# Second attention of a two-layer decoder: the product of probabilities and values issued half a step later, ahead of the next transposes

## The chip, the cores and the metric

The kernel runs on one core of one Trainium2 chip. The metric is the device time of one execution in microseconds (us). Everything is computed in 32-bit floating point. The engines are written as the profile names them: PE (TensorE, matmuls), PEld (its weight loads), DVE (VectorE), ACT (ScalarE), POOL (GpSimd) and SP (SyncE, which here issues all DMAs of the part that matters).

## What is computed

Four blocks follow each other, each with a residual and a layer norm: a first attention (low-rank, 32 heads), a gated feed-forward block, a second attention, and a linear layer with eight routed low-rank experts. The activations are 4 sequences of 256 rows, 512 wide. The change lies in the second attention:

```python
q = einsum('bsd,de->bse', x, wq).reshape(B, S, 32, 192)[..., :128]
kv = einsum('bsd,de->bse', x, wkv)            # keys and values, 32 heads of 128
scores = einsum('bqhd,bkhd->bhqk', q, k) * 192 ** -0.5
scores = where(causal, scores, -1e30)
probs = softmax(scores, axis=-1)
attn = einsum('bhqk,bkhd->bqhd', probs, v).reshape(B, S, 4096)
out = einsum('bse,ed->bsd', attn, wo)
```

## The kernel before

**Three kinds of work share the second attention.** (1) The projections to queries, keys and values and the output projection are done by a fast block scheme: seven products of blocks in place of eight, at two levels, so that each product is followed by additions. A *stage* is one group of seven products; `seven` (L787) turns it into seven *units*. A unit is a few matmuls (L874 for queries and keys, L969 for values, L1059 for the output projection) into one of three PSUM banks `ps_b`, and one eviction of that bank, on ACT (L800) or on DVE (L803; L1068 for the output projection). Later additions of whole blocks, which read the intermediate results kept in `x`, run on POOL (L895). The differences of weight blocks are made on POOL too (L136 to L139, and for the output projection L1034 to L1037). (2) The attention itself runs in 128 *steps*, one for each of 32 heads and 4 sequences. (3) DMAs, all issued in order by SP.

**A step of the attention** has five parts.

- `scores1` (L1093): two products of queries and keys into the bank `ps_s`. They are issued through the helper `mm`, so their line is L63. Then DVE adds the mask (L1100) and takes two maxima (L1104), and ACT takes two exponentials with their sums (L1108).
- `softmax1` (L1116): DVE takes the reciprocals of the sums (L1118), ACT scales the probabilities `pr` (L1120).
- `transposes1` (L1123): PE turns three 128x128 blocks of `pr` into the bank `ps_t` (L1126), and DVE copies them to `pT` (L1128).
- `output1` (L1131): PE multiplies the values `v` with `pT` into the bank `ps_o` (L1135 and L1136), ACT copies the result to `att` (L1138), and SP stores it to the DRAM buffer `attd` (L1139).
- Between these, the units that the step has been given. Heads are taken in 8 groups of 4, so a group has 16 steps. While group g is in its steps, the units of the projections of group g+1 are spread over 32 half steps (`todo`, L1221 to L1224). In the last group the units are the rest of the projections (L874), and then the first two rounds of the output projection (`so[0]` and `so[1]`, L1059).

In each step the loop (L1218 to L1244) issues: the scores of this step; the units of the first half; the transposes of the step before; the units of the second half; the product with the values of the step before; the scaling of this step's probabilities.

**The order on each engine.** The framework that builds the kernel puts the instructions of each engine into one fixed order ahead of time. It goes by the order of the code and by when it expects operands and buffers to be ready. So an instruction can stand somewhat earlier or later in an engine's queue than in the code. At run time every queue is worked off in that order.

**Buffers that matter.** `ps_s` and `ps_t` have two banks each, `ps_o` has one. `pT` has two buffers, `pr` and `att` have three. The values `v` have two buffers, so that `att0`, the buffer that later takes the attention output back for the output projection, takes the place of `v[6]`, the values of the last group but one (heads 24 to 27).

**The handover in the last group.** After the first step of the last group, the loop calls `o_load(0)` (2 MB from `attd` into `att0`, L1022), the weight loads of the first two rounds (L836 into `ws`, L839 into `w`), the weight differences of round 0 (`ahead`, L1034 to L1037 on POOL, and L1044 to L1047 for the other side, in round 0 on DVE, into `to`), `o_load(1)` (into `xo`), and `back(0)`, which reads `x` back from DRAM (L1179).

```python
            for i in range(GH * B):
                h, b = GH * g + i // B, i % B
                pr, sm = scores1(h, b)
                ...
                if pending:
                    output1(pending[0], pending[1], pT)
                pending = (h, b, softmax1(pr, sm))
                if last and i == 0:
                    o_load(0)
```

Of the kernel before, what the change touches and what calls it, by code (L numbers as in the profile page):

```python
# [38 lines left out]
def tile_decoder2(ctx: ExitStack, tc: tile.TileContext, a: dict, out: bass.AP):  # L39
# [13 lines left out]
    def bank(tag, shape=(P, 512)):  # L53
        return ps["pool"].tile(list(shape), F32, tag=tag, name=f"ps_{tag}", bufs=ps["bufs"][tag])
# [112 lines left out]
    with tc.tile_pool(name="l0", bufs=1) as l0, tc.tile_pool(name="l0b", bufs=2) as l0b:  # L167
# [280 lines left out]
        pending, flush = [], []  # L448
# [313 lines left out]
    with banks("ps1", b0=1, b1=1, b2=1, s=2, t=2, o=1), \  # L762
# [249 lines left out]
        def o_load(r):  # L1012

            if r == 0:
                ov[0] = l1.tile([P, GH, N], F32, tag="v", name="att0")
                xo = l1x.tile([P, 5 * GH, Q], F32, tag="x2o", name="xo")
                ov[1] = xo[:, :4 * GH].rearrange("p (h t) c -> p h (t c)", t=4)
                odd = [xo[:, 4 * GH:], *(wts.tile([P, 4, Q], F32, tag=f"x2{i}", name=f"xo{i}", bufs=1) for i in (2, 0))]
                ov["c"] = ([
                    l1x.tile([P, 2, HN], F32, tag=f"t{i}", name=f"to{i}") for i in (1, 3, 5)  # L1020
                ], [t.rearrange("p (h t) c -> p h (t c)", t=2) for t in odd])
            nc.sync.dma_start(out=ov[r % 2], in_=attd[r])  # L1022
# [70 lines left out]
        def scores1(h, b):  # L1093

            sc = bank("s", (P, 3, P))
            q0, q1 = bass.ts(2 * b, P), bass.ts(2 * b + 1, P)
            mm(sc[:, 0, :], [(qn[h][:, q0], kn[h][:, q0])])
            mm(sc[:, 1:3, :], [(qn[h][:, q1], kn[h][:, b * S:(b + 1) * S])])
            diag = sc[:, 0:3:2, :]
            nc.vector.tensor_tensor(diag, diag, mask, ALU.add)  # L1100
            nmx = small.tile([P, 2], F32, name="nmx")
            parts = (slice(0, 1), slice(1, 3))
            for qt, pt in enumerate(parts):
                nc.vector.tensor_reduce(nmx[:, qt:qt + 1], sc[:, pt, :], AX.XY, ALU.max, negate=True)  # L1104
            pr = l1.tile([P, 3, P], F32, tag="pr", name="pr", bufs=3)
            sm = small.tile([P, 2], F32, name="sm")
            for qt, pt in enumerate(parts):
                nc.scalar.activation(  # L1108
                    pr[:, pt, :], sc[:, pt, :], AF.Exp, bias=nmx[:, qt:qt + 1],
                    accum_out=sm[:, qt:qt + 1],  # L1110
                )
            if b == B - 1:
                free.extend((where[(True, h)], where[(False, h)]))
            return pr, sm

        def softmax1(pr, sm):  # L1116
            rc = small.tile([P, 2], F32, name="rc")
            nc.vector.reciprocal(rc, sm)  # L1118
            for qt, pt in enumerate((slice(0, 1), slice(1, 3))):
                nc.scalar.activation(pr[:, pt, :], pr[:, pt, :], AF.Copy, scale=rc[:, qt:qt + 1])  # L1120
            return pr

        def transposes1(pr):  # L1123
            tp = bank("t", (P, 3, P))
            for i in range(3):
                nc.tensor.transpose(tp[:, i, :], pr[:, i, :], ident)  # L1126
            pT = l1.tile([P, 3, P], F32, tag="pT", name="pT")
            nc.vector.tensor_copy(pT, tp)  # L1128
            return pT

        def output1(h, b, pT):  # L1131
            g, hh = divmod(h, GH)
            hv = slice(hh * DV, (hh + 1) * DV)
            po = bank("o", (P, S))
            nc.tensor.matmul(po, v[g][:, 2 * b, hv], pT[:, 0:2, :], start=True, stop=False)  # L1135
            nc.tensor.matmul(po[:, P:], v[g][:, 2 * b + 1, hv], pT[:, 2, :], start=False, stop=True)  # L1136
            att = l1.tile([P, S], F32, tag="att", name="att", bufs=3)
            nc.scalar.copy(att, po)  # L1138
            nc.sync.dma_start(out=attd[g][:, hh, b * S:(b + 1) * S], in_=att)  # L1139
# [36 lines left out]
        def back(t0):  # L1176

            for t in (t0, t0 + 2):
                nc.sync.dma_start(out=x[:, t:t + 2, :], in_=xd[:, t:t + 2, :])  # L1179
# [22 lines left out]
        def units_of(stages):  # L1202

            units = []
            for st in stages:
                def begin(st=st):
                    for key in ("load", "att", "next"):
                        if key in st:
                            st[key]()

                (u, w), rest = st["units"][0], st["units"][1:]
                units += [((lambda begin=begin, u=u: (begin(), u())), w), *rest]
            return units

        for u, _ in units_of(groups[0]):
            u()
        pending = None
        for g in range(NG):  # L1218
            last = g == NG - 1
            units = units_of(rest + so[0] + so[1]) if last else units_of(groups[g + 1])  # L1220
            total, at, todo = sum(w for _, w in units), 0, {}  # L1221
            for u, w in units:
                todo.setdefault((2 * at + w) * 4 * GH * B // (4 * total), []).append(u)
                at += w  # L1224
            for i in range(GH * B):
                h, b = GH * g + i // B, i % B
                pr, sm = scores1(h, b)
                for u in todo.get(2 * i, ()):
                    u()
                if pending:  # L1230
                    pT = transposes1(pending[2])
                for u in todo.get(2 * i + 1, ()):
                    u()
                if pending:
                    output1(pending[0], pending[1], pT)
                pending = (h, b, softmax1(pr, sm))
                if last and i == 0:
                    o_load(0)
                    even.extend((free.pop(0), free.pop(0)))
                    for r in range(2):  # L1240
                        so[r][0]["w"]()
                    so[0][0]["ahead"]()
                    o_load(1)
                    back(0)  # L1244
        output1(pending[0], pending[1], transposes1(pending[2]))


        iscale = 1.0 / math.sqrt(DK)
# [162 lines left out]
```

## Time and profile before

| what | value |
|---|---|
| time, median of 3 runs | 1682.19 us (1681.59 to 1682.57) |
| time of the profiled execution | 1681.63 us |
| its span, first to last instruction | 1679.6 us |
| mean granted clock of TensorE | 0.997 |
| steps of groups 0 to 6, up to the handover | about 880 to 1342 us of the span |
| handover in the last group | about 1342 to 1400 us |
| rest of the last group's steps | about 1400 to 1453 us |

The profile is one execution. Its page gives the busy time of each engine and the chain of work that ended last, which is followed back from the end. The trace behind it also gives, for any window, the instructions in order of time (the timeline), the chain of waits in order of time, the issues of DMAs with the time until they landed, and who waited for whom. Columns of the timeline are: start in us, duration in us, engine, line, operation, output and inputs, shape, count. A matmul in 32-bit numbers shows as two instructions, so "L1135 x2" is one product of the code. Ends of matmuls are modelled by the profiler, so starts are the safer reading.

### The profile page before, as it was taken

To read this page: it belongs to the slowest core of one execution; us is meant where nothing else is said; L and a number is where in the kernel's file an instruction comes from. 1 tells how busy PE (TensorE), PEld (TensorE's weight loads), DVE (VectorE), ACT (ScalarE), POOL (GpSimd) and SP (SyncE) were. 2 spreads that over 40 slices of the span, in tenths; PEclk is the share of its full clock that TensorE was granted. 3 is DMA by queue.
4 is the path that set the end of the run, shared out by engine and by line. 5 is a ranking of instruction groups with operands and counts; after the bars stand their busy time and mean duration, and the time that the engine had idled before them with its cause. 6 is when DMAs were issued, how large, how long until landed. Compare 5 with 4: busy or idle time off the path is not lost.

```text
span 1679.6 us, 24076 instructions
## 1 busy us (share of the span) xinstructions
PE 1644.5 (98%) x7954; PEld 1294.9 (77%) x7954; DVE 1064.9 (63%) x2345; ACT 700.8 (42%) x2070; POOL 1104.5 (66%) x1330
## 2 busy tenths in 40 slices
PE   8999999999999998999999999999999999999998
PEld 5566666666488887888878888888888878888854
DVE  3577777777745536677777666666666775433454
ACT  1566666667422202111125555555555553200043
POOL 1988888881437445786667767677676777689530
PEclk9999999999999999999999999999999999999999
DMA  9465555451312002687524334253342344443000
GB/s 345 152 211 215 217 199 205 175 194 50 108 43 77 13 26 73 200 262 248 187 76 128 115 98 144 71 178 118 95 140 73 122 176 161 155 151 125 26 18 33
DMA packets 96251, 226.88 MB, mean 135 GB/s; under 512 B 10272, under 2 KB 53792, under 8 KB 90112
## 3 DMA queue, kind: packets, MB, share of 16 engines
q1 hardware_dynamic: 94464, 224.54, 38.9%
q8 instruction: 63, 1.03, 0.3%
q10 hardware_dynamic: 1664, 0.81, 0.2%
q14 instruction: 60, 0.49, 0.1%
HBM read 140.38 MB, written 84.93 MB: 134 GB/s over the span
## 4 chain that ended last, share of the span: by engine, by line
PE 88%; DVE 7%; POOL 2%; DMA 1%; ACT 1%; issue 1%; DVEq 0%; SPq 0%; POOLq 0%; ACTq 0%
PE ps_b L874 19%; PE ps_s L63 13%; PE ps_b L1059 11%; PE ps_b L969 5%; PE ps_o L1135 4%; PE ps_o L396 3%; PE ps_s L612 3%; PE ps_t L379 3%; PE ps_p L294 3%; PE ps_t L1126 2%; PE ps_o L63 2%; PE ps_t L969 2%; PE ps_o L612 2%; PE ps_p L612 2%; PE ps_b L63 2%; PE ps_p L302 2%
## 5 line engine op out<-in xcount | busy, mean ns | idle before, releaser
L1108 ACT ACTIVATE pr<-ps_s,nmx 128x128 f32<-128x128 f32 (+1 forms) x256 | 105.0, 416 | 105.0 <-DVE nmx L1104 101.9
L355 ACT ACTIVATE pr<-ps_s,ebias 128x256 f32<-128x256 f32 x256 | 117.7, 472 | 48.5 <-DVE ebias L350 46.9
L1068 DVE TENSOR_TENSOR x<-ps_b,x 128x512 f32<-128x512 f32 x96 | 66.2, 690 | 105.0 <-PE ps_b L1059 97.5
L63 PE MATMUL ps_s<-kT,qh 128*128 128x256 f32 x512 | 129.1, 393 | 1.1 <-ACT pr L355 1.1
L1120 ACT ACTIVATE pr<-pr,rc 128x128 f32<-128x128 f32 (+1 forms) x256 | 103.8, 448 | 56.6 <-DVE rc L1118 55.0
L1100 DVE TENSOR_TENSOR ps_s<-ps_s,mask 128x256 f32<-128x256 f32 x128 | 55.2, 431 | 106.5 <-PE ps_s L63 106.5
L63 PEld LDWEIGHTS ps_s<-kT,qh 128*128 128x128 f32 x512 | 91.5, 189 | 37.6 <-issue 20.2
L803 DVE SCALAR_TENSOR_TENSOR x<-ps_b,p 128x512 f32<-128x512 f32 (+1 forms) x159 | 96.3, 607 | 22.9 <-PE ps_b L874 13.3
L344 DVE TENSOR_REDUCE nmx<-ps_s 128x2 f32<-128x512 f32 x128 | 84.9, 683 | 25.1 <-PE ps_s L63 24.2
L136 POOL TENSOR_TENSOR ws<-ws 128x128 f32<-128x128 f32 (+1 forms) x128 | 70.7, 567 | 45.6 <-DMA ws<-in_wq 27.4
L370 DVE TENSOR_SCALAR pr<-pr,rc 128x256 f32<-128x256 f32 x192 | 93.9, 515 | 4.4
L1078 POOL TENSOR_TENSOR x<-x,po 128x512 f32<-128x512 f32 x48 | 60.1, 1267 | 37.0 <-DVE x L1068 28.7
L1135 PE MATMUL ps_o<-pT,v 128*128 128x256 f32 x256 | 82.4, 404 | 0.6 <-DVE pT L1128 0.6
L1104 DVE TENSOR_REDUCE nmx<-ps_s 128x1 f32<-128x128 f32 (+1 forms) x256 | 79.4, 351 | 3.8
L1128 DVE COPY pT<-ps_t 128x384 f32<-128x384 f32 x128 | 70.3, 549 | 10.7 <-PE ps_t L1126 10.3
L800 ACT ACTIVATE p<-ps_b 128x512 f32<-128x512 f32 (+1 forms) x78 | 43.1, 552 | 75.3 <-PE ps_b L874 43.8
L396 PEld LDWEIGHTS ps_o<-pT,cN 128*64 128x64 f32 x512 | 31.8, 136 | 54.8 <-issue 22.3
L803 DVE SCALAR_TENSOR_TENSOR x<-ps_b,x 128x512 f32<-128x512 f32 (+1 forms) x106 | 64.2, 606 | 15.3 <-PE ps_b L874 8.7
L396 PE MATMUL ps_o<-pT,cN 128*64 128x256 f32 x512 | 69.4, 391 | 3.0 <-DVE pT L383 2.6
L139 POOL TENSOR_TENSOR ws<-ws,ws 128x128 f32<-128x128 f32 (+1 forms) x128 | 70.4, 564 | 2.4
L138 POOL TENSOR_TENSOR ws<-ws 128x128 f32<-128x128 f32 (+1 forms) x128 | 70.8, 567 | 1.3
L137 POOL TENSOR_TENSOR ws<-ws 128x128 f32<-128x128 f32 (+1 forms) x128 | 70.1, 563 | 1.3
(692 smaller groups left out, 4616.7 us busy)
## 6 DMA issues: line engine op xcount, KB each, us to landing
attd<-att SPq DMA_DIRECT2D x128, 128.0 KB, 1.8
vw<-ws SPq DMA_DIRECT2D x56, 256.0 KB, 2.4
qd<-ws SPq DMA_DIRECT2D x56, 256.0 KB, 2.3
qb<-vw SPq DMA_DIRECT2D x28, 512.0 KB, 4.4
qb<-qd SPq DMA_DIRECT2D x24, 512.0 KB, 4.4
v<-vd SPq DMA_DIRECT2D x6, 2048.0 KB, 8.0
qc<-vw SPq DMA_DIRECT2D x28, 384.0 KB, 3.9
vw<-ws SPq DMA_DIRECT2D x24, 384.0 KB, 2.5
```

Source lines behind the costliest of these rows:

```text
L63: nc.tensor.matmul(o, l, r, start=(i == 0), stop=(i == len(pairs) - 1))
L355: nc.scalar.activation(pr[:, i, qt, :], sc[:, qt, :], AF.Exp, bias=bias[:, i, qt:qt + 1], accum_out=sm[:, i, qt:qt + 1],)
L370: nc.vector.tensor_scalar(prs, prs, rc[:, i, qt:qt + 1], None, ALU.mult)
L396: nc.tensor.matmul(po[i * RKV:(i + 1) * RKV, :], cN[:, 2 * b + kt, :], pTs[i][:, kt, :], start=(kt == 0), stop=(kt == 1),)
L612: nc.tensor.matmul(banks_of[tag], lhs[i][:, k, :], rhs[i][:, k, :], start=first and k == 0, stop=k == 1, skip_group_check=True,)
L803: nc.vector.scalar_tensor_tensor(o[key], acc, scale, o[other], ALU.mult, ALU.add)
L874: nc.tensor.matmul(acc[:, e, :], pr.inner[i][k], inner[i][k], start=first and e == 0, stop=True, skip_group_check=True,)
L969: nc.tensor.matmul(acc[:, t, :].rearrange("p (h c) -> p h c", h=2), inner[i][k][:, t * P:(t + 1) * P], pr.inner[i][k], start=first and t = ...
L1059: nc.tensor.matmul(st[tag][:, tt, :], box["left"][i][:, k, (t0 + tt) * P:(t0 + tt + 1) * P], box["right"][i][:, k, :], start=first and tt ...
L1108: nc.scalar.activation(pr[:, pt, :], sc[:, pt, :], AF.Exp, bias=nmx[:, qt:qt + 1], accum_out=sm[:, qt:qt + 1],)
L1120: nc.scalar.activation(pr[:, pt, :], pr[:, pt, :], AF.Copy, scale=rc[:, qt:qt + 1])
L1135: nc.tensor.matmul(po, v[g][:, 2 * b, hv], pT[:, 0:2, :], start=True, stop=False)
```

## The change

The product with the values keeps what it computes and goes to another place in the loop. A second variable, `turned_`, carries the transposed probabilities of one step into the next. In each step the loop then issues: the scores of this step; the units of the first half; the product with the values of the step before the last; the transposes of the step before; the units of the second half; the scaling. After the loop two products are left in place of one. The block of calls at the handover (`o_load(0)` to `back(0)`) moves from after the first step of the last group to after the second, because the last product that reads `v[6]` is now issued in that second step.

```diff
-        pending = None
+        pending = turned_ = None
...
                 for u in todo.get(2 * i, ()):
                     u()
+                if turned_:
+                    output1(*turned_)
                 if pending:
-                    pT = transposes1(pending[2])
+                    turned_ = (*pending[:2], transposes1(pending[2]))
                 for u in todo.get(2 * i + 1, ()):
                     u()
-                if pending:
-                    output1(pending[0], pending[1], pT)
                 pending = (h, b, softmax1(pr, sm))
-                if last and i == 0:
+                if last and i == 1:
                     o_load(0)
...
-        output1(pending[0], pending[1], transposes1(pending[2]))
+        output1(*turned_)
+        output1(*pending[:2], transposes1(pending[2]))
```

## Prediction, on record before the result

> **What bounds the kernel now.** I read the page first, then the busy times of the stretch in question, then the chain of waits, and then the timeline inside one step. Part 1 of the page and the window of the steps up to the handover:
>
> ```profile
> PE 1644.5 (98%) x7954; PEld 1294.9 (77%) x7954; DVE 1064.9 (63%) x2345; ACT 700.8 (42%) x2070; POOL 1104.5 (66%) x1330
> 880.00:1342.00 462.00, 462.00 (x2440) 400.13 (x2439) 322.35 (x789) 262.21 (x845) 339.86 (x394) 1.00 0.36 116
> ```
>
> PE is shown busy for 462.00 of 462 us (the columns of the second line are PE, PEld, DVE, ACT, POOL, clock, DMA share, GB/s). The list of waits has no entry for PE there. By this reading a reordering of PE's work can bring nothing. But the ends of matmuls are modelled, so a short wait can be hidden inside a busy bar. The Trainium skill ("Perfetto Trace Analysis", Identifying the Most-Contended Engine) says that matmul busy time is no measure of the room left, because matmuls are pipelined, and that weight-load busy time is better. By matmul busy time the gain of the loop would be 0; weight loads are 400.13 of 462 us, which leaves room. Neither number is used below.
>
> Starts settle it. The chain of waits, first in a middle step, then (last line) in the last group:
>
> ```profile
> 1003.30 0.33 PE ps_t L1126 x3
> 1003.63 0.87 PE ps_b L874 x4
> 1004.50 0.22 PE ps_s L63 x2
> 1004.72 0.60 PE ps_o L1135 x2
> 1005.31 0.22 PE ps_o L1136 x2
> ...
> 1404.20 0.43 PE ps_o L1135 x2
> ```
>
> The same product of `v` and `pT` holds the chain for 0.60 us in one place and 0.43 in the other. Why, the timeline of that step shows:
>
> ```profile
> 1003.95 0.55 DVE L1128 COPY pT<-ps_t 128x384 f32<-128x384 f32 x1
> 1004.33 0.38 PE L63 MATMUL ps_s<-slot_(False, 7)_7588,slot_(True, 7)_7242 128*128 128x128 f32 x2
> 1004.64 0.67 PE L1135 MATMUL ps_o<-pT,v 128*128 128x256 f32 x2
> 1005.15 0.38 PE L1136 MATMUL ps_o<-pT,v 128*128 128x128 f32 x2
> ```
>
> The copy of `pT` ends at 1004.50; the product starts 0.14 later. The scores' matmul before it takes 0.22, so it could have started at 1004.55: 0.09 lost. The next matmul then starts 0.51 after it, against 0.43 between unhindered ones of that shape: another 0.08. Wherever `pT` was ready 0.26 us ahead, the pair took 0.43 and nothing was lost.
>
> **The sum, part by part.**
>
> *The loop, up to the handover.* I took the start of every PE instruction from 880 to 1342 us and subtracted full speed (0.216 us for a 128x256 instruction, 0.11 for a 128x128 one). There are 105 products with the values. 76 wait for `pT`: together they lose 6.1 us before they start and 5.9 us inside the pair, **12.0 us**, 0.158 each; 29 lose nothing. The chain of waits agrees: its 105 pieces of L1135 last 57.0 us, against 105 x 0.43 = 45.2. After the change `pT` is copied half a step or more before its product, about 2 us, against the 0.26 that was enough. So I take all of it: -12.0. The bounds are 0 (a like wait appears elsewhere in the step) and -12.0.
>
> *Cover for a unit.* Twice in each group, 12 times up to 1342, a one-head unit (L874) stands 0.02 late and is stretched by about 0.10 us, with a DVE eviction (L803) ending just ahead. The transposes (0.33 us) are then its only cover; the moved product adds 0.65 in the same place. That is 12 x 0.12 = -1.4, between 0 and -1.4.
>
> *What follows the product.* The ACT copy (L1138, 0.37 us) and the store on SP (L1139) are issued about half a step later. `ps_o` has one bank, but its next use is still a whole step, about 4.4 us, later. The last product on each `v` moves too: the 2 MB load that waits for it lands in a median of 8.0 us and is first used a whole group later, about 70 us. Cost 0; without that cover it would be a load of 8 us, six times. The transposes come 0.65 us later, so the scaled `pr`, ready 1.7 to 2.3 us ahead in the steps I read, has more time.
>
> *The handover.* Here PE isn't the bound. From 1342.4 to 1372.2 the chain runs on POOL, and then:
>
> ```profile
> 1370.90 1.27 POOL slot_(False, 31)_11830 L895
> 1372.17 0.02 issue
> 1372.19 0.32 SPq L1179
> ...
> 1372.60 8.47 DMA att<-attd
> 1381.07 0.02 issue
> 1381.10 0.79 DVE to L1044
> ...
> 1384.32 2.04 DVE to L1046
> 1386.36 0.04 issue
> 1386.40 3.72 PE ps_b L1059 x16
> ```
>
> POOL's additions release `x`, SP passes its DMA of `x`, the 2 MB load of `att0` is issued at 1372.60, and the output projection waits for it and for DVE behind it. The 0.5 us that products lose inside the POOL stretch gain nothing: PE stands still for 2.25 us at 1371.65 anyway. What is late next is `att0`. It takes over the buffer of `v[6]`, whose last reader, today done by 1369.9, will stand behind the four units of the second step's first half. The last of these starts at 1373.90, after that standstill. Add 0.44 for it, 0.65 for the product and 0.1 to 0.2 for the issue: about 1375.2, **2.6 us later** than 1372.60. In SP's queue stand behind this load the weight load (L839), the load of `xo`, the store (L1139) and the reads of `x`; round 1, which needs the first two, starts at 1415 with its POOL work done by 1400.6, so they have some 15 us to spare. The 2.6 us aren't all lost: in this stretch the queue of PE already runs ahead with scores and transposes, and the product that is put off (0.65 us) fills part. I subtract that and a little more, 0.8: **+1.8**. The bounds are 0 (all filled) and +2.6 from this; for a worse queue order see the second rival. A wait of 0.87 us of one product for `pT` at 1378 may go as well; I leave it in the range.
>
> *After the loop.* One product of 0.65 us is issued after the last step instead of inside it. It is the same work, with units of the output projection on both sides. 0.
>
> Sum: -12.0 - 1.4 + 1.8 = **-11.6**. The profiled execution took 1681.63 us (span 1679.6, 2.0 around it), so 1670.0 on its scale; it lies 0.56 below the median of the runs shown, so 1670.6. I say 1671.
>
> **The rivals.**
>
> *Nothing changes (chance 0.10).* PE's bar is solid, and the lost 0.158 us could belong to the instruction and not to the wait, or turn up at the transposes. Then only the handover moves the time: 1682.2 + 0 to 2.6, about 1683.5. Against it: 102 of the 105 products have the same separate wait instruction in PE's queue, and 29 of the 105 lose nothing.
>
> *The handover takes back half (chance 0.14).* If the load of `att0` stands in SP's queue behind the two last reads of `x` (L1179), which wait for POOL's addition at 1377.76 to 1379.0 and take 0.6 us each to issue, it goes out at about 1380.3 instead of 1372.6. Of these 7.7 us PE can fill perhaps 2: the sum is -12.0 - 1.4 + 5.7, about 1674.5; with little filled, 1677. For it: the queue before already has one such read ahead of the load. Against it: the load comes first in the code.
>
> *Slower (chance 0.08).* ACT works in order. If the copy of the product (L1138) is put ahead of this step's exponentials, these wait for a product that now ends in mid step. In the step at 1000.75 the exponentials start 2.04 us after the scores; the copy would end at 0.66 + 1.73 (units) + 0.65 + 0.2 + 0.37 = 3.6, so they come 1.6 us later. DVE's reciprocals then hold up the evictions behind them, by up to about 0.3 us a step: 105 x 0.3 = +31, less 13, about 1700. It decides from 0.13 us a step (13.4 / 105), where the gain is gone; at 0.16 the kernel is slower by 0.2%. Against it: the queues follow readiness (the first matmul of the next scores was pulled ahead of the waiting product), and the scaled `pr` has its 1.7 us to spare.
>
> **How the numbers follow.** The forecast has 0.68: 1666.5 to 1674, with all of the loop's gain and a handover of -2 to +3. The second rival takes the range to 1677; to 1678 covers a cover gain of 0 besides. So 1666.5 to 1678 holds 0.82. A change of 0.2% (3.4 us) is about what a measurement of this kernel can tell from none. Faster by more: 0.68 + 0.14 = 0.82; within: 0.10; slower: 0.08.
>
> **What would show it.** In the changed profile the pieces of L1135 in the chain last 0.43 us in all groups, the next start follows by 0.43, and a step of the loop takes about 0.12 us less on average. `att<-attd` is issued some 2.6 us later against POOL's last additions (L895) than now, and PE's waits around it grow by 1 to 3 us. I am wrong if the L1135 pieces keep 0.55 to 0.60, if the transposes (L1126) or units (L874) take over such a stretch, or if the scores are followed by later exponentials.

## The result, and the profile after

| | median | lowest to highest | profiled execution | its span |
|---|---|---|---|---|
| before | 1681.89 us (4 runs) | 1678.11 to 1682.57 | 1681.63 | 1679.6 |
| after | 1665.97 us (4 runs) | 1663.24 to 1668.65 | 1663.24 | 1661.4 |

The ratio is **0.9903** (95% interval 0.9889 to 0.9918): 16 us faster (13.8 to 18.7), where 11.6 were forecast.

Part 1 of the page and the window of the undisturbed steps, of after:

```profile
PE 1628.2 (98%) x7954; PEld 1298.1 (78%) x7954; DVE 1074.5 (65%) x2345; ACT 694.1 (42%) x2070; POOL 1104.7 (66%) x1330
```

```profile
880.00:1330.00 450.00, 450.00 (x2449) 405.98 (x2449) 330.06 (x792) 257.14 (x847) 341.89 (x402) 1.00 0.36 119
```

PE's bar is as solid as before, 450.00 of 450 us. But the same work now fits a shorter stretch: 2449 PE instructions in 450 us, where before had 2440 in 462. The bar itself says nothing of the gain. The chain of waits of after, in a middle step:

```profile
1002.57 1.73 PE ps_b L874 x8
1004.30 0.43 PE ps_o L1135 x2
1004.73 0.22 PE ps_o L1136 x2
1004.95 0.33 PE ps_t L1126 x3
1005.28 1.30 PE ps_b L874 x6
1006.58 0.66 PE ps_s L63 x4
```

The product (L1135) takes 0.43 where it took 0.60, and what follows it takes no longer than its share: 0.22, then 0.33 for the transposes. The `pT` that it reads was copied in the step before, from 1001.1 to 1001.7, some 2.5 us earlier than PE starts on it.

**Where the time went.** I cut both traces at events that they share: the first transposes of the loop, POOL's last weight difference before the handover (L136, `cc<-c`), the first unit of the output projection that reads `to` (L1059), and the last product with the values (L1135).

| stretch, us | before | after | difference |
|---|---|---|---|
| start to first transposes | 884.1 | 880.9 | -3.2 |
| to POOL's last L136 (the loop) | 458.2 | 444.3 | -13.9 |
| to the first unit that reads `to` | 44.0 | 45.5 | +1.5 |
| to the last product | 65.4 | 62.9 | -2.5 |
| to the end | 227.8 | 227.8 | 0 |

The first row isn't the change's: its code and PE's order in it are the same. In the executions profiled for this study it lies anywhere from 880.9 to 888.4 us. So the two spans (18.2 apart) overstate the gain by about 3. The stretches that the change touches give -13.9 + 1.5 - 2.5 = **-14.9**, within the measured interval.

**The handover.** The chain of after, from POOL's last additions on:

```profile
1353.16 1.26 POOL slot_(False, 31)_11824 L895
1354.42 1.23 POOL slot_(True, 30)_11487 L895
1355.67 0.44 DVE x L803
1356.15 0.70 PE ps_b L874 x2
1356.85 0.43 PE ps_o L1135 x2
...
1368.56 2.14 DVE to L1046
1370.74 5.45 PE ps_b L1059 x24
```

The DMA of `att0`, which held this chain for 8.47 us before, is no longer in it: from 1356 on, PE's own work and the softmax of its steps fill the time until DVE has made `to`. The margin is small: the load lands at 1365.37, and DVE starts on it at 1365.74. In the other profiled execution of the change (change_again, below) DVE starts 0.02 us after the landing. SP's queue in the same place:

```profile
1357.54 0.32 SPq L1022 DMA_DIRECT2D att<-attd  x1
1357.95 0.38 SPq L1139 DMA_DIRECT2D attd<-att  x1
1358.73 0.33 SPq L839 DMA_DIRECT2D w<-in_wo  x1
1359.11 0.54 SPq L1022 DMA_DIRECT2D xo<-attd  x1
1360.20 1.54 SPq L1179 DMA_DIRECT2D x<-xd  x2
```

The load is issued 3.16 us after POOL starts its addition into `slot_(True, 30)` (1354.38), where it was 0.48 (1372.12 to 1372.60): 2.7 later, as forecast (2.6). The two last reads of `x` stand behind it, so the rival of the worse queue order is out. But PE loses less here, not more. Its standstills over 0.5 us, ahead of the first unit that reads `to`, were 2.25, 0.87, 0.56 and 0.78; they are 1.80 and 0.51. All lost time between POOL's last L136 and that unit, by starts against full speed, falls from 5.6 to 3.9 us.

### The profile page after: what moved, and what is told of

The parts are those of the page before. It is cut to its first block, busy times and chain, and to the rows that moved or that the text cites. A ratio compares the mean times of both kernels' runs of the same rounds, so it can differ in the third digit from the quotient of the medians.

```text
span 1661.4 us, 24088 instructions
## 1 busy us (share of the span) xinstructions
PE 1628.2 (98%) x7954; PEld 1298.1 (78%) x7954; DVE 1074.5 (65%) x2345; ACT 694.1 (42%) x2070; POOL 1104.7 (66%) x1330
## 4 chain that ended last, share of the span: by engine, by line
PE 91%; DVE 6%; ACT 1%; POOL 1%; issue 1%; DMA 1%; DVEq 0%; ACTq 0%; POOLq 0%
PE ps_b L874 20%; PE ps_s L63 14%; PE ps_b L1059 11%; PE ps_b L969 5%; PE ps_o L396 4%; PE ps_o L1135 3%; PE ps_s L612 3%; PE ps_t L379 3%; PE ps_p L294 3%; PE ps_t L1126 2%; PE ps_o L63 2%; PE ps_t L969 2%; PE ps_o L612 2%; PE ps_p L612 2%; PE ps_p L302 2%; PE ps_b L63 2%
## 5 line engine op out<-in xcount | busy, mean ns | idle before, releaser
L1108 ACT ACTIVATE pr<-ps_s,nmx 128x128 f32<-128x128 f32 (+1 forms) x256 | 105.0, 416 | 141.9 <-DVE nmx L1104 141.8
L1120 ACT ACTIVATE pr<-pr,rc 128x128 f32<-128x128 f32 (+1 forms) x256 | 103.5, 454 | 13.9 <-DVE rc L1118 13.0
L136 POOL TENSOR_TENSOR ws<-ws 128x128 f32<-128x128 f32 (+1 forms) x128 | 70.4, 566 | 44.2 <-DMA ws<-in_wq 25.7
L1135 PE MATMUL ps_o<-pT,v 128*128 128x256 f32 x256 | 76.3, 380 | 0.1
```

The source lines that it names most:

```text
L1108: nc.scalar.activation(pr[:, pt, :], sc[:, pt, :], AF.Exp, bias=nmx[:, qt:qt + 1], accum_out=sm[:, qt:qt + 1],)
```

## The experiments

**Theory.** The gain is the wait for `pT` in the loop: a product needs about 0.26 us of cover behind its copy, wherever it stands. The handover's later load costs nothing because PE has other work. **Rivals:** the gain comes from the place (ahead of the transposes); it comes from the last group; or the late load does cost 2 us, and something else gave more than it seems.

Each kernel was timed beside before, in 4 to 12 runs. The table has what was measured; "handover" is from POOL's last L136 to the last product.

| kernel | median us | ratio (95%) | loop | handover |
|---|---|---|---|---|
| before (profile above) | | | 458.2 | 109.4 |
| after (profile above) | | | 444.3 | 108.4 |
| change_again | 1665.89 | 0.9909 (0.9896 to 0.9923) | 444.3 | 107.8 |
| loop_only | 1669.29 | 0.9921 (0.9903 to 0.9939) | 444.3 | 108.9 |
| last_only | 1681.77 | 1.0002 (0.9992 to 1.0012) | 458.3 | 108.3 |
| early_release | 1668.84 | 0.9919 (0.9905 to 0.9934) | 444.3 | 108.3 |
| old_place_older | 1674.14 | 0.9959 (0.9945 to 0.9974) | 446.0 | 113.3 |
| behind_scores | 1667.02 | 0.9916 (0.9902 to 0.9929) | 445.3 | 107.7 |
| change_copy_twice | 1671.75 | 0.9948 (0.9935 to 0.9960) | 444.3 | 114.2 |
| before_copy_twice | 1676.00 | 0.9969 (0.9957 to 0.9981) | 449.3 | 111.9 |

Before itself had medians of 1681.45 (23 runs, beside loop_only, last_only, early_release and old_place_older) and 1681.97 (10 runs, beside the others). All diffs are against after, unless they say otherwise.

**loop_only**: the new order in groups 0 to 6; the last group as before, its handover too.

```diff
                 if turned_:
                     output1(*turned_)
+                    turned_ = None
                 if pending:
                     turned_ = (*pending[:2], transposes1(pending[2]))
...
+                if last:
+                    output1(*turned_)
+                    turned_ = None
                 pending = (h, b, softmax1(pr, sm))
-                if last and i == 1:
+                if last and i == 0:
...
-        output1(*turned_)
         output1(*pending[:2], transposes1(pending[2]))
```

> New order in groups 0 to 6, old order and old handover in the last group. Theory now: the loop gives 13.4 us and the handover stays as it was, so about 13.5 us faster than before, and some 1.5 to 2 us slower than the whole change. The forecast on record had the handover cost 1.8, by which this kernel would be 1.8 us faster than the whole change.

**last_only**: the opposite; the old order in groups 0 to 6, the new one and the later handover in the last group.

```diff
                 if turned_:
                     output1(*turned_)
+                    turned_ = None
...
                 for u in todo.get(2 * i + 1, ()):
                     u()
+                if turned_ and not last:
+                    output1(*turned_)
+                    turned_ = None
```

> Old order in groups 0 to 6, new order and late handover in the last group. Theory now: att0 is issued 2.6 us later than before but PE's queue runs ahead by two more steps, and its idle time from the POOL stretch to the second product of round 0 falls by 1.5 us: 1.5 to 2 us faster than before. By the forecast on record 1.8 us slower. If the difference in the handover was only a faster DMA in that one execution, 0 to 2.6 slower.

Measured: the loop's gain is all in loop_only (444.3 against 458.2), and last_only has none of it. By the times loop_only is 13.3 us faster than before (10.3 to 16.3).

The new handover on its own is shorter too. With the old loop and the same products in it, it takes 108.3 us (last_only) against 109.4 (before). With the new loop, where one product more falls into it, it takes 108.4 and 107.8 (after, change_again) against 108.9 (loop_only). No run sees it lose 2 us. By the times last_only lies between 1.3 us faster and 2.0 us slower than before, so the 1.5 to 2 us that I expected didn't come; the 1.1 us of the trace is too small to see there.

The two kernels also show where PE loses its time between POOL's last L136 and the first unit that reads `to` (in us, by starts against full speed):

| kernel | ahead of the standstill behind POOL | this standstill | behind it |
|---|---|---|---|
| before | 0.4 | 2.2 | 3.0 |
| loop_only | 0.0 | 1.4 | 3.1 |
| last_only | 0.6 | 2.2 | 1.7 |
| after | 0.2 | 1.8 | 1.9 |

The new order of the loop shortens the standstill (by 0.9 us alone, by 0.4 with both), and the new order of the last group, its later load included, takes away more than 1 us of the losses behind it.

**early_release**: in the second step of the last group the waiting product goes ahead of the first half's units, so that `v[6]` comes free earlier.

```diff
                 pr, sm = scores1(h, b)
+                if last and i == 1:
+                    output1(*turned_)
+                    turned_ = None
                 for u in todo.get(2 * i, ()):
```

> The change, but in the second step of the last group the last product on v[6] goes ahead of the units of the first half, so that att0 can be loaded before the standstill for POOL. If the late load still costs something, att0 is issued about 2.5 us earlier and this is 1 to 2.5 us faster than the change; if PE fills the wait with steps run ahead, the same within 0.5 us.

Measured: SP's queue of this kernel shows the load 1.0 us after POOL starts its addition (1361.80):

```profile
1362.76 0.38 SPq L1022 DMA_DIRECT2D att<-attd  x1
```

The first unit that reads `to` comes 1.4 to 1.8 us earlier than in after and change_again, and the rest takes 1.7 to 1.8 longer: 43.7 + 64.6 = 108.3 in place of 108.4 and 107.8. By the times it is 13.6 us faster than before (11.1 to 16.0), so no faster than the change. **The later load costs nothing here.** Ahead of the first unit with `att0`, and behind POOL's standstill, PE's queue holds the scores of 4 steps and 2 products here; in after it holds 5 and 4, and before it held 3 and 2. What is done there need not be done later.

**change_again**: the change itself, beside behind_scores and the two kernels that copy twice.

> The change itself once more, beside before on the same chip. The segments of the runs so far say 13.9 us less up to the handover and 1.0 less from there to the last product, nothing after: 14.9 us faster than before. The first measurement gave 16.2 (its interval about 14 to 19).

Measured: as the first time, with 444.3 and 107.8. The stretches from the first transposes to the last product are 15.5 us shorter than those of before, where after had 14.9; the time is 15.3 us less (13.0 to 17.5).

**behind_scores**: the product directly behind the scores, ahead of the units of the first half.

```diff
                 pr, sm = scores1(h, b)
-                for u in todo.get(2 * i, ()):
-                    u()
                 if turned_:
                     output1(*turned_)
...
+                for u in todo.get(2 * i, ()):
+                    u()
```

> The change, with the product of the step before the last directly behind the scores, ahead of the units of the first half. If the wait for pT is the main thing and place only matters as cover for the one-head units, the stretch up to the handover takes some 446 us as with the old place (444.3 in the change, 458.2 before), with the 0.1 us stretches of the one-head units back; about 13 us faster than before. If the place ahead of the transposes matters more, it is much nearer to before.

**old_place_older**: the product stays in its old place behind the second half's units, but is that of the step before the last.

```diff
-                if turned_:
-                    output1(*turned_)
+                ready_ = turned_
                 if pending:
                     turned_ = (*pending[:2], transposes1(pending[2]))
                 for u in todo.get(2 * i + 1, ()):
                     u()
+                if ready_:
+                    output1(*ready_)
```

> The product with the values takes the pT of the step before the last, as in the change, but keeps its old place behind the second half's units. If the gain of the loop comes from the wait for a fresh pT, no product is stretched (L1135 to L1136 0.43 us everywhere) and 12 us of the 13.4 stay, only the 1.4 us of the one-head units come back: about 13 to 15 us faster than before with the handover. If it comes from the place (between units and transposes, more even cover for evictions), the time is within 3 us of before.

Measured: the age of `pT` is what counts. In the loop behind_scores is 0.9 us and old_place_older 1.7 us slower than after; no product loses time in either, wherever it stands. In behind_scores the youngest `pT` is 0.39 us old when its product starts. In before, the 76 products that lost time had one of 0.15 us or less, and the 29 that lost none had 0.27 or more. The place is worth the small rest: in old_place_older the one-head units (L874) are uncovered again and lose 1.24 us in sum, nearly what the forecast had for them (1.4). In behind_scores they lose nothing, against what I had expected; 0.65 of its 0.9 us is one product more ahead of POOL's last L136. By the times behind_scores is 14.1 us faster than before (11.9 to 16.5), which can't be told from the change.

old_place_older is only 6.9 us faster (4.4 to 9.2), not the 13 to 15 expected: the loop is 12.2 us shorter than in before, but the handover is 3.9 us longer.

The handover of old_place_older is 4.9 us longer than that of after. There the load of `att0` waits for a product that now stands behind two halves of units (SP's queue has it at 1365.21, 7.1 us after the start of POOL's addition, not 3.2). And PE runs slower for a while (columns as in the windows above; the clock is the third number from the end):

```profile
1358.00:1360.00 2.00, 0.08 (x1) 0.08 (x1) 0.56 (x3) 0.38 (x1) 2.00 (x3) 1.00 0.49 106
1360.00:1362.00 2.00, 1.94 (x7) 1.38 (x8) 1.62 (x5) 0.92 (x4) 0.63 (x1) 0.67 0.61 221
1362.00:1364.00 2.00, 2.00 (x6) 1.55 (x6) 0.58 (x3) 0.40 (x1) 1.03 (x1) 0.50 0.00 0
```

After a standstill of 2.15 us the granted clock falls to 0.50 for about 3.4 us, in which a pair of L1135 takes 0.85 (1.7 us lost). What the load, 3.9 us later than in after, has to do with the other 3.2 isn't shown: it isn't in the chain of waits there, which runs through PE and the softmax of steps run ahead. So that a load is free was seen for 2.7 us, not for more.

**change_copy_twice** and **before_copy_twice**: the copy of `pT` is made twice, in after and in before, so that it is ready about 0.5 us later. The line numbers behind it shift by one.

```diff
             nc.vector.tensor_copy(pT, tp)
+            nc.vector.tensor_copy(pT, tp)
```

> The change, with the copy of the transposed probabilities to pT done twice on DVE, which keeps the result. pT comes some 0.5 us later, and DVE has 60 us more work. If the change has taken the copy off PE's path, the stretch up to the handover stays at 444 to 447 us, at most 3 us slower than the change.

> Before, with the copy done twice. If the product waits for the copy, the stretch up to the handover grows from 458.2 us; the framework now puts both scores and sometimes a unit ahead of the product, which hides a part of it: 3 to 30 us slower than before. If the lost 0.158 us were a matter of the instruction and not of the copy, it stays within 2 us of before.

Measured: in after the loop doesn't see it, 444.3 as without. What it costs, 5.8 us where I had allowed 3, it costs in the handover, where DVE with its second copies stands in the chain, PE stands still for 3.25 us, and the clock then falls to 0.50 for some 3.4 us.

In before I was wrong about the sign: it became 5.2 us *faster* (3.2 to 7.2). The chain of waits of before_copy_twice says how:

```profile
1002.41 0.86 PE ps_b L874 x4
1003.28 0.66 PE ps_s L63 x4
1003.93 0.43 PE ps_b L874 x2
1004.36 0.43 PE ps_o L1136 x2
1004.79 0.22 PE ps_o L1137 x2
```

PE's order is another one. Before, one of the two products of the scores stood ahead of the product with `v`; here both do, and often a unit as well. So the later `pT` is in time: all the loop's products together lose 0.2 us before they start and 4.0 inside the pair, where before lost 6.1 and 5.9. The order is fixed ahead of time by when operands are expected to be ready. That the second copy moved this expectation is my inference; the new order and the shorter waits are in the trace. It also shows what before suffered from: not from a `pT` that can't be had in time, but from an order that puts the product 0.1 to 0.2 us too early.

None of these kernels beats the change.

## Why the prediction was right, and where it was wrong

**What bounds the kernel: right.** The loop was PE-bound with its loss hidden in a solid bar. The bar stayed solid and the loop became 13.9 us shorter.

**The products that wait for `pT`, -12.0: right, at the upper bound as taken.** Nothing took the wait's place at the transposes or units, and in the changed loop no product loses time before it starts or inside the pair. The page's group of this line shows a part of it, the busy time in a modelled bar; before and after:

```profile
L1135 PE MATMUL ps_o<-pT,v 128*128 128x256 f32 x256 | 82.4, 404 | 0.6 <-DVE pT L1128 0.6
```

```profile
L1135 PE MATMUL ps_o<-pT,v 128*128 128x256 f32 x256 | 76.3, 380 | 0.1
```

It falls by 6.1 us (404 to 380 ns each): that is the loss inside the pairs, 5.9. The other half, ahead of the pairs, is in no group of the product; it was counted as busy time of whatever stood before it. Only starts show both.

**The units' cover, -1.4: right.** With the product in that place the loss is gone; in old_place_older it is back (1.24).

With one product (0.65) put off past the end of the loop the terms give -12.0 - 1.4 - 0.65 = -14.05; the cut shows -13.9.

**The handover, +1.8: wrong, and this is the step that failed.** The forecast said: "The 2.6 us aren't all lost: in this stretch the queue of PE already runs ahead with scores and transposes, and the product that is put off (0.65 us) fills part. I subtract that and a little more, 0.8: +1.8." The 2.6 was right (2.7 measured), the filling was not 0.8. By the cut the handover takes 1.0 us less, and that holds the product that was put off; like for like it is -1.7, so the term was off by 3.5 us. PE's lost time ahead of the first unit that reads `to` was to grow by 1 to 3 us and fell by 1.7 (5.6 to 3.9). What stands in its place: PE had lost 2.2 us behind POOL's stretch already (0.87, 0.56 and 0.78), in waits for `pT`, for `att0` and for `to`. In PE's timeline of before (the number in brackets is the idle time that the profile shows ahead of the instruction):

```profile
1373.90 0.70 PE L874 MATMUL ps_b<-x,cc 128*128 128x256 f32 x2 [2.08 <-DVE x L803]
1379.25 0.70 PE L1135 MATMUL ps_o<-pT,v 128*128 128x256 f32 x2 [0.65 <-DVE pT L1128]
1381.21 1.97 PE L1059 MATMUL ps_b<-ws,att 128*128 128x256 f32 x8 [0.38 <-DMA att<-attd]
1386.40 1.99 PE L1059 MATMUL ps_b<-cu,to 128*128 128x256 f32 x8 [0.56 <-DVE to L1046]
```

The same four places in after:

```profile
1356.15 0.70 PE L874 MATMUL ps_b<-x,cc 128*128 128x256 f32 x2 [1.64 <-DVE x L803]
1361.09 0.67 PE L1135 MATMUL ps_o<-pT,v 128*128 128x256 f32 x2
1366.10 1.89 PE L1059 MATMUL ps_b<-ws,att 128*128 128x256 f32 x8
1370.74 1.99 PE L1059 MATMUL ps_b<-cu,to 128*128 128x256 f32 x8 [0.27 <-DVE to L1046]
```

In after the product starts 0.26 late in place of 0.87, nothing waits for the load, and two more scores and two more products stand ahead of it. So there is about 3.2 us more work ahead of the first unit that reads `to` (1.5 us more time and 1.7 less lost). I had bounded this term by 0 below, as all filled, and named only the 0.87 as a possible gain, "in the range" and not in the sum. early_release confirms that the lateness has no price: earlier by most of it, no faster. Of the 1.7 us, 1.1 are the losses behind the standstill; last_only has this gain and loop_only hasn't, so it belongs to the new order of the last group.

A smaller part, 0.4 us, is the standstill behind POOL: 1.80 in place of 2.25. The stretch from POOL's last L136 to its addition into `slot_(True, 30)` is 0.6 us shorter, and with it both loads of `ws` go out together at 1328.55 (before, a store stood between them), and POOL waits 3.0 us for them, not 4.1. The new order of the loop alone does this: loop_only, where the call is in its old place, has the two loads together and waits 3.0 us too, while last_only has the store between them, waits 3.7 and keeps a standstill of 2.2. The forecast had no term for it.

**The range.** It was worked out as 1666.5 to 1678; the median is 1665.97, 0.5 us below it. Its low end had all of the loop's gain and a handover of -2 against the median of before; the loop's gain and the measured handover give -14.9 in after and -15.5 in change_again, at 1667.3 and 1666.7 on that scale. So the handover term moved the time from the 1671 of the forecast close to the low end, and about a microsecond on top of that is not accounted for. The interval (13.8 to 18.7) allows it and no run here pins it down; the second timing of the change gave 15.3 (13.0 to 17.5). The low end left no room for such a spread, though the median of before alone lay between 1681.45 and 1682.19. The 1674 of the narrower range doesn't follow from the terms named for it either: 1682.2 - 13.4 + 3 is 1671.8.

**The rivals.** That nothing changes is out by the time. The queue order that takes half back is out by SP's order. The copy (L1138) ahead of the exponentials didn't come: in the step at 1002 of after, the exponentials (L1108) run from 1003.79, the copy follows at 1004.99, and from 885 to 1330 us the chain of waits of after holds pieces of PE alone.

## What to carry to other kernels

A solid PE bar can hide a short wait in every step: compare start-to-start times of the same instruction in several places, and multiply the difference by the steps. Where an engine's order is fixed ahead of time, let a product use an operand that is half a step old instead of one just made; a few tenths of a microsecond of cover were enough here (0.27 us), and the place hardly mattered. Before pricing a later load at a handover, list the idle time that is already there and the work that can move into it: what the engine does ahead of the load need not be done after it. Where two moves are made at once, try each alone: what one of them gives can look like the other's.

## What the hardware showed that I had not expected

**Half clock after short standstills.** In three of the ten profiled executions the granted clock fell to 0.50 for about 3.4 us in the handover, 0.8 to 1.5 us after PE had ended a standstill of 2.15, 2.18 and 3.25 us. In two others it stayed at 1.00 after 2.25 and 2.23 us, and in none did it fall after 1.8 or less. The Trainium skill ("TensorE: Matmul & The Clock Gate", Part 1) says that the clock is halved after an idle window of about 3.4 us, and that this window runs freely. The length of the slow time agrees with that window; that 2.15 us of standstill were enough once, and 2.25 were not another time, suggests that where a standstill lies in the window counts, and that a window need not be idle throughout. No run here tests it.

**An unchanged front that varies.** The time up to the first transposes of the second attention, with the same code and PE order, lay between 880.9 and 888.4 us. A pair of profiles can so differ by several us without any edit: cut at shared events before comparing.
